# A convolution and expert-routing kernel on one core: smaller second matrices, normalising work spread to GpSimd, the choice of experts in two parts

## The chip, the core and the metric

The kernel runs on one core of a Trainium2 chip. The core has a matrix engine (PE; its weight loads are listed apart as PEld), VectorE (DVE in the profile), ScalarE (ACT), GpSimd (POOL) and SyncE (SP, which here only issues transfers). Each engine takes its own instructions strictly in order and waits for the others on semaphores. Transfers between the chip's memory and the on-chip memory run on 16 transfer engines; SP, ACT and POOL each have a queue that issues them.

The time is device microseconds of one execution. The metric is the median of several runs. A separate, profiled execution gives the trace.

## What is computed

The input is 32 images of 128 channels, 56 x 56. Layer 0, cut to what matters here:

```python
x = depthwise_conv7x7(input) + dw_bias            # each channel by itself
x = x.transpose(0, 2, 3, 1)                       # tokens: one per pixel, 128 channels
x = (x - mean) / sqrt(var + 1e-6) * ln_gamma + ln_beta
logits = x @ Wg + bg                              # 8 experts
topv, topi = top_k(logits, 2); wts = softmax(topv)
# tokens in order of falling wts[:, 0]; each expert keeps the first `cap` of them
h = gelu(buf @ W1 + b1); y = h @ W2 + b2          # per expert
out0 = input + x + layer_scale * (weighted sum of a token's two experts)
```

Layer 1 is a dilated 3 x 3 convolution, a two-dimensional Fourier transform, attention and a gate in the frequency domain, and the way back. The change touches nothing of it.

## The kernel before

The kernel has three parts in time: the **convolution stage** with the layer norm and the choice of experts (up to about 1073 us), the routing and the experts, and the last part with the combination and layer 1. Only the first is touched.

The convolution stage works on 8 **groups** of 4 images. A group has TG = 98 columns of 128 tokens; its result is the tile `y`, 128 tokens x 98 columns x 128 channels, of which two exist, so that one group can be finished while the next is filled. A group is filled in 16 **steps** (NS) of 8 channels (CB). Step `k` calls `conv` (L124): it loads `xt`, the pixels of 8 channels on 112 partitions (L127), and `wt`, the matrices of these channels (L129); both have three buffers. The 7 x 7 convolution of a channel is written as matrix products: 8 x 8 output pixels of a tile need 14 rows of input, which are cut into two **row blocks** of 8 rows; `b` = 0 and 1 are the two products that are added up (L136). A row block has 8 rows x 14 columns = 112 rows of a matrix (PK). In the second block, rows 6 and 7 of 8 carry only zeros. VectorE takes 4 channels at a time out of PE's result, adds the bias and writes `y` (L144): two evictions a step.

A filled group is worked off behind the steps of the next one, in seven **blocks** of columns (six of 16, one of 2). `block` (L152) has five phases:

- `stats`: VectorE's `bn_stats` per column (L161), a few small operations, ScalarE's square root (L172), reciprocal and bias (L173, L174);
- `norm`: ScalarE scales and shifts each column with its own two factors (L181), VectorE multiplies the whole block by gamma and adds beta (L185), ScalarE's queue issues the write to `xf` in memory (L188);
- `across`: PE transposes the columns (L196), ScalarE copies four at a time (L198);
- `logits`: PE multiplies by Wg (L206, L234), ScalarE copies (L215);
- `back`: PE transposes (L220), VectorE adds the bias into `lg` (L223, L243).

After the last block, `choose` (L252) finds the two largest logits of each token, in some 20 VectorE operations over all 98 columns (L263 to L302), ScalarE's exponential (L291) among them; it fills `meta`, a tile with a single buffer that GpSimd clears first (L288), and ScalarE's queue issues the write of `meta` to `xf` (L299), in pieces of 64 bytes, 12,544 of them. `key` (L302) stays on the chip.

`plan` (L314) sets the order: phase `i` of block `b` is put behind step `b * 3 // 2 + i` of the next group, and `choose` behind the step after the last phase, the fifteenth. The last group has no next one: its phases run one after another, the **tail** of the stage. After that, the order of instructions on each engine is made by the framework's scheduler, which moves instructions ahead where it finds room; waits follow from the tiles' use. PE's order keeps to the plan: the transposes of block 0 stand behind step 2 of the next group, those of blocks 1 to 6 behind steps 3, 5, 6, 8, 9 and 11. They wait for the normalised block, and the matmuls of the next step stand behind them.

The tiles of the next part lie where those of the stage lay, so its first instructions wait for the stage's last transfers; VectorE's memset of `onesj` (L470) waits for the last write of `meta`.

Of the kernel before, what the change touches and what calls it, by code (L numbers as in the profile page):

```python
# [29 lines left out]
F32 = mybir.dt.float32  # L30
I32 = mybir.dt.int32
AF = mybir.ActivationFunctionType
ALU = mybir.AluOpType
# [4 lines left out]
C = 128  # L38
# [6 lines left out]
E = 8  # L45
# [4 lines left out]
P8 = 8  # L50
NB = H // P8
NP = NB * NB
NCB = NB + 1
PK = P8 * (P8 + 6)
CB = 8
PITCH = 144
BIG = 1.0e30
# [14 lines left out]
def conv_seq_kernel(ctx: ExitStack, tc: tile.TileContext, t: dict, out: bass.AP, dbg: dict):  # L72
    nc = tc.nc
# [39 lines left out]
    TG = 2 * NP  # L113
    with tc.tile_pool(name="a1", bufs=1) as a1, tc.tile_pool(name="a2", bufs=2) as a2, tc.tile_pool(
# [9 lines left out]
        def conv(g, c0, y):  # L124

            xt = a3.tile([PK, CB, 4 * NCB * NB], F32, name="xt")
            nc.sync.dma_start(out=xt, in_=t["x8"][g, c0 // CB])  # L127
            wt = a3.tile([PK, CB, 2, P8 * P8], F32, name="wt")
            nc.sync.dma_start(out=wt, in_=t["wt"][c0 // CB])  # L129
            xv = xt.rearrange("k c (h n q) -> k c h n q", h=2, n=2)  # L130
            for c4 in range(0, CB, 4):
                ps = bank("psa")
                for c in range(4):
                    for b in range(2):
                        for h in range(2):
                            nc.tensor.matmul(  # L136
                                ps[h * 64 : (h + 1) * 64, c * TG : (c + 1) * TG],
                                lhsT=wt[:, c4 + c, b, :],
                                rhs=xv[:, c4 + c, h, :, b * NB : b * NB + NP],
                                start=(b == 0),  # L140
                                stop=(b == 1),
                            )
                cs = slice(c0 + c4, c0 + c4 + 4)
                nc.vector.tensor_tensor(  # L144
                    out=y[:, :, cs],
                    in0=ps[:, : 4 * TG].rearrange("p (c t) -> p t c", c=4),
                    in1=dwbB[:, cs].unsqueeze(1).broadcast_to([128, TG, 4]),
                    op=ALU.add,
                )

        def block(g, y, lg, t0, n):
# [26 lines left out]
            def norm():  # L178
                for i in range(n):
                    yi = y[:, t0 + i, :]  # L180
                    nc.scalar.activation(  # L181
                        yi, yi, AF.Identity, scale=sd[:, i : i + 1], bias=nb[:, i : i + 1]
                    )
                for w, op in ((gB, ALU.mult), (bB, ALU.add)):
                    nc.vector.tensor_tensor(  # L185
                        out=yb, in0=yb, in1=w.unsqueeze(1).broadcast_to([128, n, C]), op=op
                    )
                nc.scalar.dma_start(out=xfv[:, g * TG + t0 : g * TG + t0 + n, :C], in_=yb)  # L188
# [60 lines left out]

            return [stats, norm, across, logits, back]  # L250

        def choose(g, lg):  # L252

            cut = slice(g * TG, (g + 1) * TG)
            bE = [128, TG, E]
            tops, hots = [], []
            cand = a1.tile(bE, F32, name="cand", tag="cand")
            for r in range(2):

                top = a2.tile([128, TG], F32, name=f"top{r}", tag=f"top{r}")  # L260
                first = firsts[r][:, cut]
                hot = a1.tile(bE, F32, name=f"hot{r}", tag=f"hot{r}")
# [24 lines left out]
            meta = a1.tile([128, TG, PITCH - C], F32, name="meta", tag="meta")  # L287
# [26 lines left out]
        def plan(g, y):  # L314
# [907 lines left out]
def layouts(np, v):  # L1222
# [34 lines left out]
    def bn(v, g, b, m, bias):  # L1257
# [2 lines left out]
    return {  # L1260
        "xp": xp,
        "x8": x8.reshape(n // 4, C // CB, PK, CB, 4 * NCB * NB),
        "wt": wt.reshape(C // CB, PK, CB, 2, P8 * P8),
        "iota": np.arange(128 + n // 2 * NP, dtype=f),
        "reset": np.tile((np.arange(NB) > 0).astype(f), n // 2 * NB),
        "dw_bias": L0["dw_bias"],
# [41 lines left out]
```

## Time and profile before

| | us |
|---|---|
| median of 3 runs | 6502.28 (6499.15 to 6507.23) |
| the profiled execution | 6513.53 |
| its span in the trace | 6511.8 |
| PE busy (matmuls) | 4898.1 (75%) |
| VectorE busy | 3096.6 (48%) |
| GpSimd busy | 2601.1 (40%) |
| ScalarE busy | 2097.7 (32%) |
| first matmul of the convolution stage | at 12.41 |
| last eviction of the convolution stage | at 944.18 |
| end of the last write of `meta` | at 1073.25 |

Busy times are sums over an engine's instructions; a share of the whole span is a mean over parts with different limits, so each part has to be read by itself. The page cuts the span into 40 slices of about 163 us and prints the busy share of each in tenths. A timeline gives, for each piece: start, duration, engine, source line, operation, written tile and read tiles, count, and in brackets the idle time before it with what ended it. A wait is listed as "engine, tile, line <- what ended it: us in total, times, longest". The granted clock of PE in the stage is about 0.8 of full speed.

In the stage, per instruction: a matmul of L136 264 ns (mean), an eviction 565 ns, a ScalarE activation of one column 489 ns (one starts every 0.39 us), a VectorE multiplication or addition of a block of 16 columns 2290 and 2278 ns, a `bn_stats` 289 ns, a clearing of `meta` 1405 ns.

### The profile page before, as it was taken

How to read it: one execution, taken by the hardware profiler on the slowest of the kernel's cores; microseconds unless marked ns; L12 is line 12 of the kernel's file. 1: busy time of each engine (PE TensorE's matmuls, PEld its weight loads, DVE VectorE, ACT ScalarE, POOL GpSimd, SP SyncE). 2: the span in 40 equal slices, each digit the busy share in tenths (PEclk: the TensorE clock that was granted, in tenths of full speed). 3: DMA queues.
4: the chain of work that ended last, by engine and by line, in shares of the span. 5: the costliest groups of instructions: out<-in, count | busy, mean ns of one | idle time of the engine just before them, and what ended most of it. 6: DMA issues, size and time to landing. Idle time of an engine off the chain costs nothing.

```text
span 6511.8 us, 85508 instructions
## 1 busy us (share of the span) xinstructions
PE 4898.1 (75%) x32850; PEld 3362.9 (52%) x32850; DVE 3096.6 (48%) x6927; ACT 2097.7 (32%) x3595; POOL 2601.1 (40%) x2564
## 2 busy tenths in 40 slices
PE   6666652699898989999965677777777677767778
PEld 5555542476576756776742344443444444344445
DVE  4676675565665655535311343344344344434335
ACT  2445442133232323333310332233333233333225
POOL 0000000335343434544446555455555555655540
PEclk8878875799898999999986888888878888888889
DMA  8998973122121222222232233333333333323331
GB/s 230 224 227 221 231 186 75 45 62 69 50 69 52 69 55 68 71 67 71 73 110 59 63 91 89 83 92 81 83 93 89 85 94 96 84 72 96 88 86 43
DMA packets 616217, 634.09 MB, mean 97 GB/s; under 512 B 166145, under 2 KB 540546, under 8 KB 611714
## 3 DMA queue, kind: packets, MB, share of 16 engines
q1 hardware_dynamic: 332418, 395.64, 22.0%
q0 software_dynamic: 81664, 175.18, 11.7%
q10 hardware_dynamic: 201728, 57.81, 4.6%
q8 instruction: 260, 4.26, 0.3%
q14 instruction: 147, 1.20, 0.1%
HBM read 454.98 MB, written 173.41 MB: 97 GB/s over the span
## 4 chain that ended last, share of the span: by engine, by line
PE 36%; issue 15%; another core or an unknown queue 13%; POOL 8%; DVE 6%; DMA 2%; ACT 2%; DVEq 0%; POOLq 0%; SPq 0%; ACTq 0%
PE pf L895 8%; PE py L715 8%; PE ph L705 7%; POOL xg L671 6%; PE pm L939 6%; PE pt L931 3%; POOL y L850 2%; DMA xg<-xf,ids 2%; PE pg L964 2%; DVE mid L933 1%; PE pre L1030 1%; PE pim L1031 1%; PE pxt L677 1%; PE pxs L872 1%
## 5 line engine op out<-in xcount | busy, mean ns | idle before, releaser
L850 POOL DMA_INDIRECT y<-yf,slot x1568 | 1628.5, 1039 | 1403.0 <-DVE xs L864 764.8
L671 POOL DMA_INDIRECT xg<-xf,ids x984 | 961.1, 977 | 1380.9 <-PE pxt L677 519.7
L708 ACT ACTIVATE hT<-ph,b1t 128x512 f32<-128x512 f32 (+1 forms) x992 | 672.9, 682 | 1455.6 <-PE ph L705 1294.6
L715 PEld LDWEIGHTS py<-W,hT 128*128 128x128 f32 x7872 | 949.0, 194 | 241.0 <-issue 122.8
L895 PE MATMUL pf<-xp,cw 128*64 128x448 f32 x4032 | 988.2, 595 | 110.7 <-issue 69.5
L715 PE MATMUL py<-W,hT 128*128 128x128 f32 x7872 | 998.0, 281 | 88.9 <-DVE gat L682 42.0
L705 PE MATMUL ph<-xT,W 128*128 128x512 f32 (+1 forms) x1984 | 910.2, 597 | 8.8 <-issue 8.1
L933 DVE COPY mid<-pt 112x512 f32<-112x512 f32 (+3 forms) x480 | 312.6, 663 | 940.5 <-remote 413.3
L895 PEld LDWEIGHTS pf<-xp,cw 128*64 128x64 f32 x4032 | 315.8, 147 | 622.8 <-issue 547.7
L705 PEld LDWEIGHTS ph<-xT,W 128*128 128x128 f32 x1984 | 360.2, 194 | 349.9 <-issue 344.2
L136 PE MATMUL psa<-xt,wt 112*64 112x98 f32 x8192 | 416.5, 264 | 86.6 <-DMA wt<-in_wt_dram 80.9
L136 PEld LDWEIGHTS psa<-xt,wt 112*64 112x64 f32 x8192 | 392.9, 147 | 125.2 <-issue 59.4
L682 DVE SCALAR_TENSOR_TENSOR gat<-xg 128x4 f32<-128x4 f32 (+2 forms) x256 | 42.2, 165 | 763.9 <-DMA xg<-xf,ids 763.1
L288 POOL MEMSET meta<- 128x1568 f32 x8 | 11.2, 1405 | 951.1 <-DMA xf<-meta 360.8
L196 PE MATMUL pyt<-ident,y 128*128 128x128 f32 x784 | 154.3, 377 | 305.3 <-DVE nb L174 148.4
L877 DVE TENSOR_TENSOR xp<-xp,pxs 128x256 f32<-128x256 f32 x448 | 147.2, 385 | 489.0 <-remote 348.3
L942 ACT COPY T<-pm 128x464 f32<-128x464 f32 (+2 forms) x240 | 123.7, 520 | 617.1 <-PE pm L939 367.2
L939 PE MATMUL pm<-rh,mid 112*128 112x116 f32 x928 | 142.1, 298 | 236.5 <-issue 161.0
L181 ACT ACTIVATE y<-y,nb,sd 128x128 f32<-128x128 f32 x784 | 311.0, 489 | 18.5 <-DVE nb L174 18.5
L196 PEld LDWEIGHTS pyt<-ident,y 128*128 128x128 f32 x784 | 138.3, 201 | 331.8 <-issue 239.6
L864 DVE TENSOR_TENSOR xs<-xs,y 128x896 f32<-128x896 f32 x224 | 242.2, 1087 | 116.7 <-DMA y<-yf,slot 68.6
L144 DVE TENSOR_TENSOR y<-psa,dwbB 128x392 f32<-128x392 f32 x256 | 144.1, 565 | 317.0 <-PE psa L136 316.5
(376 smaller groups left out, 6498.0 us busy)
## 6 DMA issues: line engine op xcount, KB each, us to landing
xt<-in_x_dram SPq DMA_DIRECT2D x128, 784.0 KB
yf<-yo SPq DMA_DIRECT2D x240, 256.0 KB
xp<-in_xp_dram SPq DMA_DIRECT2D x32, 1832.0 KB
wt<-in_wt_dram SPq DMA_DIRECT2D x128, 448.0 KB
xs<-xf SPq DMA_DIRECT2D x112, 448.0 KB
xf<-y ACTq DMA_DIRECT2D x48, 1024.0 KB
y<-yf,slot POOLq DMA_INDIRECT x1568
out_dram<-oa SPq DMA_DIRECT2D x224, 112.0 KB
```

What stands on the lines that cost most here:

```text
L136: nc.tensor.matmul(ps[h * 64 : (h + 1) * 64, c * TG : (c + 1) * TG], lhsT=wt[:, c4 + c, b, :], rhs=xv[:, c4 + c, h, :, b * NB : b * NB + N ...
L181: nc.scalar.activation(yi, yi, AF.Identity, scale=sd[:, i : i + 1], bias=nb[:, i : i + 1])
L196: nc.tensor.transpose(pt[:, i * 128 : (i + 1) * 128], y[:, t0 + i0 + i, :], ident)
L671: nc.gpsimd.indirect_dma_start(out=xg[:n, q, :], out_offset=None, in_=xf, in_offset=bass.IndirectOffsetOnAxis(ap=ids[:n, c0 + q : c0 + q + ...
L705: nc.tensor.matmul(ph[:, :ns], lhsT=W1[:, e, f * C : (f + 1) * C], rhs=xT[:, :ns], start=True, stop=True)
L708: nc.scalar.activation(hT[:, f, :ns], ph[:, :ns], AF.Gelu, bias=b1t[:, e, f : f + 1])
L715: nc.tensor.matmul(py[:n, q * C : (q + 1) * C], lhsT=hT[:, f, q * 128 : q * 128 + n], rhs=W2[:, e, f, :], start=(f == 0), stop=(f == FF // ...
L850: nc.gpsimd.indirect_dma_start(out=y[:, m, :], out_offset=None, in_=yf, in_offset=bass.IndirectOffsetOnAxis(ap=s[:, r * NB + m : r * NB + ...
L864: nc.vector.tensor_tensor(out=xs, in0=xs, in1=y, op=ALU.add)
L895: nc.tensor.matmul(pf[i * DD : (i + 1) * DD, : 8 * W], lhsT=cw[:, k, :], rhs=xps[i][:, o : o + 8 * RP].rearrange("p (h w) -> p h w", w=RP) ...
L933: dve(mid[:m, :ni, :].rearrange("p i c -> p (i c)"), pt[:m, : ni * 128])
L939: nc.tensor.matmul(pm[:, i * M : (i + 1) * M], lhsT=mid[:m, i, :], rhs=by, start=True, stop=True)
```

## The change

It has three parts.

1. The matrices are two tensors, `wt0` with 112 rows and `wt1` with the 84 rows that are not all zero; each step loads both, and the second product uses 84 partitions of `xt`. A step's loads fall from 784 + 448 KB to 784 + 224 + 168 KB, in three transfers instead of two.
2. In `norm`, columns 1, 4, 7, 10 and 13 of a block (5 of 16; 1 in the last block of 2) are scaled and shifted by GpSimd instead of ScalarE, and the addition of beta is GpSimd's instead of VectorE's. The multiplication by gamma stays on VectorE, between the two.
3. `choose` is called twice a group: for the first three blocks (48 columns) behind step 8, for the other four (50 columns) behind step 14. Each call clears and writes its own part of `meta`; the tile has one buffer as before.

```diff
-            wt = a3.tile([PK, CB, 2, P8 * P8], F32, name="wt")
-            nc.sync.dma_start(out=wt, in_=t["wt"][c0 // CB])
+            wts = []
+            for b, k in enumerate(PKS):
+                wt = a3.tile([k, CB, P8 * P8], F32, name=f"wt{b}")
+                nc.sync.dma_start(out=wt, in_=t[f"wt{b}"][c0 // CB])
+                wts.append(wt)
...
-                                lhsT=wt[:, c4 + c, b, :],
-                                rhs=xv[:, c4 + c, h, :, b * NB : b * NB + NP],
+                                lhsT=wts[b][:, c4 + c, :],
+                                rhs=xv[: PKS[b], c4 + c, h, :, b * NB : b * NB + NP],
...
-                    nc.scalar.activation(
-                        yi, yi, AF.Identity, scale=sd[:, i : i + 1], bias=nb[:, i : i + 1]
-                    )
-                for w, op in ((gB, ALU.mult), (bB, ALU.add)):
-                    nc.vector.tensor_tensor(
+                    si, bi = sd[:, i : i + 1], nb[:, i : i + 1]
+                    if i % 3 == 1:
+                        nc.gpsimd.tensor_scalar(
+                            out=yi, in0=yi, scalar1=si, scalar2=bi, op0=ALU.mult, op1=ALU.add
+                        )
+                    else:
+                        nc.scalar.activation(yi, yi, AF.Identity, scale=si, bias=bi)
+                for w, op, eng in ((gB, ALU.mult, nc.vector), (bB, ALU.add, nc.gpsimd)):
+                    eng.tensor_tensor(
                         out=yb, in0=yb, in1=w.unsqueeze(1).broadcast_to([128, n, C]), op=op
                     )
...
-        def choose(g, lg):
+        def choose(g, lg, t0, t1):
...
-            last = max(at)
-            at[last + 1] = [lambda: choose(g, lg)]
+            half = sum(sizes[:3])
+            at.setdefault(8, []).append(lambda: choose(g, lg, 0, half))
+            at.setdefault((len(sizes) - 1) * 3 // 2 + 5, []).append(lambda: choose(g, lg, half, TG))
```

PE's order of products and transposes in the stage stays as it was, up to the tail. GpSimd, which had nothing in the stage but one clearing a group, now has in each group: the clearing of the second half's `meta`, the clearing of the next first half's, the five activations of block 0, its addition, those of block 1, its addition, ten activations (blocks 2 and 3), two additions, eleven activations (blocks 4 to 6), three additions. On VectorE most of the first half's choice stands between the multiplications of blocks 4 and 5. On ScalarE the write of the first half's `meta` is issued just before block 5's write of `y`.

More of the change, by code (lines that the diff above doesn't have):

```diff
@@ L54 @@
 PK = P8 * (P8 + 6)
+PKS = PK, 6 * (P8 + 6)
 CB = 8
@@ L250, in block @@
             return [stats, norm, across, logits, back]
-        def choose(g, lg):
-            cut = slice(g * TG, (g + 1) * TG)
-            bE = [128, TG, E]
+        def choose(g, lg, t0, t1):
+            n = t1 - t0
+            lg = lg[:, t0:t1, :]
+            cut = slice(g * TG + t0, g * TG + t1)
+            bE = [128, n, E]
             tops, hots = [], []
-            cand = a1.tile(bE, F32, name="cand", tag="cand")
+            cand = a1.tile([128, TG, E], F32, name="cand", tag="cand")[:, :n]
             for r in range(2):
-                top = a2.tile([128, TG], F32, name=f"top{r}", tag=f"top{r}")
+                top = a2.tile([128, TG], F32, name=f"top{r}", tag=f"top{r}")[:, :n]
                 first = firsts[r][:, cut]
-                hot = a1.tile(bE, F32, name=f"hot{r}", tag=f"hot{r}")
+                hot = a1.tile([128, TG, E], F32, name=f"hot{r}", tag=f"hot{r}")[:, :n]
                 nc.vector.tensor_reduce(out=top, in_=lg, axis=AX.X, op=ALU.max)
@@ L286, in choose @@
             m1, e1 = tops
-            meta = a1.tile([128, TG, PITCH - C], F32, name="meta", tag="meta")
+            meta = a1.tile([128, TG, PITCH - C], F32, name="meta", tag="meta")[:, :n]
             nc.gpsimd.memset(meta, 0.0)
@@ L1262, in layouts @@
         "x8": x8.reshape(n // 4, C // CB, PK, CB, 4 * NCB * NB),
-        "wt": wt.reshape(C // CB, PK, CB, 2, P8 * P8),
+        "wt0": wt[..., 0, :, :].reshape(C // CB, PK, CB, P8 * P8),
+        "wt1": wt[:, :6, ..., 1, :, :].reshape(C // CB, PKS[1], CB, P8 * P8),
         "iota": np.arange(128 + n // 2 * NP, dtype=f),
```

## The prediction

> **What bounds the kernel now.** I read the page's slices first, then the busy time by window, then the waits of the first 800 us, then the timeline of one period of the convolution stage. The built program is the old one after that stage, but for line numbers and a little order at its edge, so all gain or loss lies before 1073 us.
>
> ```profile
> DVE  4676675565665655535311343344344344434335
> ...
> DMA  8998973122121222222232233333333333323331
> ```
>
> The first five slices (163 us each) are the stage: the transfer engines are nearly full there and nowhere else, VectorE stands at about seven tenths. Close up, by windows of 100 us (columns: busy time of PE, weight loads, VectorE, ScalarE, GpSimd; granted clock; transfer share):
>
> ```profile
> 300.00:400.00 100.00, 64.44 (x978) 56.22 (x974) 71.41 (x211) 40.38 (x96) 1.41 (x1) 0.81 0.99 227
> 400.00:500.00 100.00, 62.46 (x950) 55.28 (x950) 71.80 (x198) 43.78 (x104) 1.40 (x1) 0.79 0.99 231
> ```
>
> No compute engine is full and the transfers look full, which suggests a stage bound by loads. The waits say otherwise:
>
> ```profile
> PE pyt L196 <- DVE nb L174: 100.6, 18, 13.3
> ...
> PE psa L136 <- DMA wt<-in_wt_dram: 71.2, 38, 12.4
> ...
> PE pyt L196 <- ACT y L181: 39.3, 5, 7.9
> ```
>
> PE waits longer for normalised rows (the transposes of L196) than for loads. The period from 336.8 to 459.4 us shows how both fit. After the last eviction of a group (336.83) come three loaded steps; then PE stands before the transposes of block 0 (they start at 362.67), and again before those of blocks 1 to 5, at 380.03, 391.98, 405.63, 418.81 and 428.88. Meanwhile the three buffers fill up and SP stops issuing (transfers fall to zero near 377 and 385 us). Steps 10 to 13 then run at PE's pace, and PE waits for loads only from 449.96 on, some 2 us a step. So a period is a **chain of blocks** (92 us) plus a stretch in which loads decide (30 us). The last link of the chain, word for word:
>
> ```profile
> 418.81 1.94 PE L196 MATMUL pyt<-ident,y 128*128 128x128 f32 x16 [1.02 <-DVE y L185]
> ...
> 423.64 0.57 DVE L144 TENSOR_TENSOR y<-psa,dwbB 128x392 f32<-128x392 f32 x1 [0.78 <-PE psa L136]
> 424.13 2.28 DVE L185 TENSOR_TENSOR y<-y,gB 128x2048 f32<-128x2048 f32 x1
> ...
> 426.44 2.29 DVE L185 TENSOR_TENSOR y<-y,bB 128x2048 f32<-128x2048 f32 x1
> ...
> 428.88 3.65 PE L196 MATMUL pyt<-ident,y 128*128 128x128 f32 x16 [4.29 <-DVE nb L174]
> ```
>
> Block 4's transposes, a step of matmuls, its two evictions, multiplication, addition, block 5's transposes: the addition stands in the chain with its full 2.29 us.
>
> **The addition on GpSimd.** No row shows GpSimd adding. Its memset of 128x1568 takes 1405 ns, 0.90 ns an element, so 2048 elements cost 1.84 us for one stream; two operands in and one out cost 5.5 us if streams follow each other. Bounds 1.84 and 5.5 us. I take 4.6, two and a half streams, since the row of its own engine is nearer than VectorE's 2.28. That is +2.3 us per block of 16. The Trainium skill's page GPSIMD Engine Reference, Performance versus the Vector engine, speaks against this move: it gives 4497 ns for this addition on GpSimd and 2293 on VectorE; the second agrees with 2.28 here, and by the first the difference would be 2.2 instead of 2.3, and the sum below 5 us smaller.
>
> **A third of the normalising.** ScalarE's row (L181, 128x128) starts one every 0.39 us; 11 instead of 16 save 1.95 us a block. GpSimd's five, at two streams of 128 and the 0.10 us of its smallest memsets, are about 0.35 each (bounds 0.2, and 0.49, ScalarE's mean), 1.75 us a block beside ScalarE.
>
> **The chain, link by link** (before, then after). *Last eviction to block 0*: 25.8. The second half's choice is half as long (below), so its meta write leaves at 337.4, not 343.88. But GpSimd's order puts the memset for the next group's first half, which waits for that write, ahead of block 0's five activations. Beside loads the write moved 7373 packets in 20 us, so 6400 need 17 us; GpSimd is free at 355.4, the five end at 357.2, multiplication 359.5, addition 364.2, transposes 364.3: 27.5. *0 to 1*: 17.4, set by copies, 16 activations (6.27), multiplication and addition. After, seven activations are left behind the copies, and the multiplication is set by the next step's evictions, at 8.0; with 2.3 and 4.7 it is 15.1. *1 to 2*: multiplication at 7.2 in both (behind L223), so 12.0 becomes 14.3. *2 to 3*: was set by 16 activations, now by an eviction at 5.4: 13.7 becomes 12.5. *3 to 4*: 13.2, plus 2.3 and a reduction of the first choice in VectorE's order: 15.6. *4 to 5*: 10.1 becomes 12.4. Sum 92.2 to 97.4: **+5.2** a period. ScalarE's relief shortens two links; in the others an eviction decides and the slower addition is paid in full.
>
> Beside the additions, VectorE now runs halves of the choice ahead of block 5's multiplication. No row has GpSimd reading tiles beside VectorE; its memsets take 1.40 us beside VectorE work as alone. Between nothing and a wait that costs 2 us (VectorE held for the addition's 4.6, less the slack in that link) I take **+0.5**; a gain is excluded, since neither engine gets less to do by it.
>
> **The loads.** One step moves 1232 KB; from 15 to 85 us, loads alone, 18.00 MB in 70 us make 4.9 us a step. 56 KB less is 0.22 us if all 16 transfer engines share it, nothing if some engine keeps seven rows. On rows of 2048 instead of 4096 bytes I put no price: the y writes, in rows of 512, run at up to 290 GB/s when alone (the slices of 960 to 1000 us), the loads at 259. About six steps a period wait for loads: -1.3 to 0. The page DMA: Bandwidth & Descriptors, Why a DMA increments its semaphore by 16 and not by 1, says that a transfer is split over the largest number up to 16 that divides its rows: 112 rows take 16 engines, 84 only 14, six rows each. By it the fullest engine falls from 78,848 to 76,800 bytes a step, 2.6% instead of 4.5%, or 0.13 us; no row here shows single engines. I take **-1.0**. SP's third issue a step (0.42 us) stands in a queue that mostly waits for PE.
>
> **The choice in two parts.** The same elements, twice the instructions: 16 more, some 0.1 us each, on a VectorE at 72% that loses 2.28 us a block. The first half's meta write moves from the chain, where transfers have gaps, into the loaded stretch. In 343 to 363 us the loads took 20 us for 17 us of work beside 7373 packets, 0.4 ns a packet: up to +2.5. Also, a y write issued behind a meta write holds ScalarE's queue:
>
> ```profile
> 343.88 0.37 ACTq L299 DMA_DIRECT2D xf<-meta  x1
> ...
> 362.60 4.34 ACTq L188 DMA_DIRECT2D xf<-y  x1
> ```
>
> 4.34 us instead of 0.37. After, block 5's y write is issued directly behind the first half's meta write, and its four copies, the logits and step 11 stand behind it: 0 to +4, partly taken up by PE's later waits. Both together, **+2.8**.
>
> Sum of a period: 5.2 + 0.5 - 1.0 + 2.8 = +7.5; seven periods +52.
>
> **The tail**, from the last eviction (944.18) to 1073.2. Block 0 is no longer behind the long choice: its transposes come 5 us earlier. The six links then lose half of that: -2.6 at block 5. The last choice took 1043.46 to 1057.29; at 0.57 instead of 0.97 us for each of its 13 large instructions it saves 6. The wait behind it,
>
> ```profile
> 1057.29 15.96 DMA xf<-meta
> ```
>
> falls with 6400 instead of 12544 packets to about 9: -7. Together **-15**.
>
> **Sum.** +52 - 15 = +37 us on the profiled 6513.53 (span 6511.8): 6550. That execution is 11 us above the median of 6502.28, so the median becomes **6540**.
>
> **Rivals.** *The addition is fast.* A microsecond of it is worth six links in seven periods and six in the tail, 48 us. Below 3.8 us the sum turns negative; at VectorE's 2.28 it would be -74, near the most that the gaps of the transfers (8 us a period) and the tail allow: 6430. For it speaks that memset's rate is no worse than VectorE's; against, that two operands must be read. 0.20. *All cancels*: the addition near 3.8, or the first half's write costs nothing: 6502. 0.10. *GpSimd is held*: its memset waits as long as now, when the whole meta write lands 24 to 26 us after its issue, so block 0 comes 8 us later still, and VectorE waits for additions: +10 a period, 6610. Against it, half the packets. 0.10. *The smaller matrices bring nothing* is inside the forecast: it costs 7 us.
>
> **Chances.** Forecast 0.60 (6516 to 6590). About 13 us, 0.2%, is what a measurement of this kernel can tell from no change. Faster 0.20, within 0.10, slower 0.70. With the addition's bounds the range is 6470 to 6600: it leaves out the fastest additions and the worst hold.
>
> **What would show it.** In the new profile: the addition's mean on GpSimd, about 4.6 us; transposes of blocks 2, 4 and 5 later after their forerunners by 2.3 us, those of 1 and 3 earlier; the period 129 us instead of 122; more transfer gaps though fewer bytes; the memset of 768 elements a microsecond or two before block 0's activations on GpSimd; block 5's y issue over 1 us; the stage's end some 37 us later, and nothing different behind it. An addition under 3.8 us, or a chain that still ends 92 us after the last eviction, makes it wrong.

## The result, and the profile after

| | us |
|---|---|
| before, median of 4 runs | 6504.75 (6499.15 to 6510.69) |
| after, median of 4 runs | 6566.01 (6549.64 to 6577.24) |
| ratio | 1.0092, 95% interval 1.0068 to 1.0116 |
| profiled execution of after, its span | 6564.6, 6562.8 |
| clearing of `onesj`, the stage's end | 1142.3 (before 1073.5) |

The change costs 61 us; 38 were forecast. The whole loss arises ahead of the stage's end, which comes 69 us later; the later parts, with the same instructions, give 18 us of it back in these two profiled executions, which are 51 us apart (by the medians it is 8 us). A second pair of runs on another chip gave 6581.52 against 6511.57, ratio 1.0105 (1.0052 to 1.0159), with the stage's end at 1147.3.

First the slices of the page of after, the counterpart of the two lines shown of before:

```profile
DVE  4767776656656555345221234443443344434336
...
DMA  8788774122222222222233233333333333333331
```

In the first five slices the transfers have fallen from eights and nines to sevens and eights: the stage moves 7 MB less and takes longer. VectorE is no less busy. By windows of 100 us (busy time of PE, weight loads, VectorE, ScalarE, GpSimd; granted clock; transfer share; GB/s), again for after:

```profile
300.00:400.00 100.00, 61.81 (x831) 54.05 (x827) 74.70 (x200) 26.96 (x60) 27.68 (x23) 0.76 0.81 195
400.00:500.00 100.00, 73.19 (x1055) 62.69 (x1056) 67.33 (x135) 33.21 (x73) 26.56 (x22) 0.83 0.81 208
```

VectorE finishes 335 instructions in 200 us, before 409, and is as busy: some of its instructions have become longer. The transfer share fell from 0.99 to 0.81. The stage now waits for its chain more than before, and the waits of the first 800 us of after say at what:

```profile
POOL meta L298 <- DMA xf<-meta: 236.7, 10, 42.1
...
PE pyt L204 <- POOL y L193: 216.6, 31, 14.9
ACT y L191 <- DVE nb L178: 152.7, 22, 13.2
...
PE psa L140 <- DMA wt<-in_wt_dram: 44.8, 37, 10.9
```

PE's transposes now wait for GpSimd's addition (L193); the wait for matrices has gone down from 71.2 to 44.8 us. New is the third line, ScalarE waiting for `nb` (L178), the bias of the next block's activations: 12 us between 200 and 900 us in before, 144 in after (15 in after with the addition back on VectorE, below).

From here, the **period** is the mean time from one group's last eviction to the next one's over the last six periods (before 121.9 us, after 134.1), and a **link** is the time from one block's transposes to the next one's. In the period of after that starts at 352.3:

| link to block | 0 | 1 | 2 | 3 | 4 | 5 | chain | behind it |
|---|---|---|---|---|---|---|---|---|
| before | 25.8 | 17.4 | 12.0 | 13.6 | 13.2 | 10.1 | 92.1 | 30.5 |
| forecast | 27.5 | 15.1 | 14.3 | 12.5 | 15.6 | 12.4 | 97.4 | 32.3 |
| after | 28.4 | 16.8 | 15.0 | 13.9 | 14.9 | 15.3 | 104.1 | 32.4 |
| before, mean of the six periods | 26.4 | 17.3 | 12.3 | 13.7 | 13.1 | 10.1 | 92.9 | 29.0 |
| after, mean of the six periods | 27.2 | 16.8 | 14.6 | 13.8 | 14.7 | 15.2 | 102.4 | 31.8 |

By the means the chain grew by 9.5 us and the stretch behind it by 2.7.

What VectorE and ScalarE do beside an addition stands in the timeline of after. Block 3's addition (421.72), its transposes (426.27) and the first of block 4's activations (426.28; start, duration, engine, line, operation, in brackets the idle time before and what ended it):

```profile
421.72 4.49 POOL L193 TENSOR_TENSOR y<-y,bB 128x2048 f32<-128x2048 f32 x1 [9.41 <-DVE y L193]
421.84 4.41 DVE L178 SCALAR_TENSOR_TENSOR nb<-nb,sd 128x16 f32<-128x16 f32 x1
...
426.27 3.62 PE L204 MATMUL pyt<-ident,y 128*128 128x128 f32 x16 [6.44 <-POOL y L193]
426.28 0.49 ACT L191 ACTIVATE y<-y,nb,sd 128x128 f32<-128x128 f32 x1 [5.72 <-DVE nb L178]
```

An operation on 16 elements takes 4.41 us instead of 0.15: VectorE starts it beside the addition and is done when the addition is done. All of VectorE's queue stands behind it, and so does ScalarE, which needs `nb`. The same happens beside each of the six additions of a period, to one operation each, by its place in VectorE's order:

```profile
408.22 4.10 DVE L170 TENSOR_TENSOR nb<-st 128x2 f32<-128x2 f32 x1
...
436.86 4.61 DVE L274 TENSOR_TENSOR cand<-lg,top 128x384 f32<-128x384 f32 x1
...
451.93 4.48 DVE L303 TENSOR_SCALAR top<-top 128x48 f32<-128x48 f32 x1
```

Not every operation is held. In the second profile of after, between 200 and 900 us, all 15 of the `nb` operations of 128x16 that met an addition took 4.4 us, the 15 others 0.15. But where the addition alone was moved (a run below, with `meta` cleared once), ten evictions lie wholly beside an addition, and took 0.50 to 0.57 as always; their first operand lies in PE's result memory. The Trainium skill's page SBUF — State Buffer, Who interferes with whom, says that a VectorE instruction with two inputs in SBUF contends with a GpSimd instruction that reads SBUF, not with one that only writes, and that the second to come waits for the whole of the first; it counts `tensor_scalar` among those that can contend too. The rows here agree with it. They show the other order too: block 5's addition, which began 0.07 us behind a VectorE operation on two tiles (128x384), took 4.83 us in all six periods, where the other blocks' took 4.49 to 4.54.

A hold lengthens the chain only where it stands on it. The chain that ended last in after, followed back from its end, shows this (start, us, engine and line; `x64` are the matmuls of a step), first in the link to block 1, then in those to blocks 3 and 5:

```profile
376.31 4.29 DVE nb L178
...
412.36 3.46 PE pyt L204 x16
415.82 3.03 PE psa L140 x64
...
419.36 2.29 DVE y L193
421.72 4.50 POOL y L193
426.27 3.62 PE pyt L204 x16
...
441.12 3.68 PE pyt L204 x16
444.79 3.87 PE psa L140 x64
...
449.17 2.29 DVE y L193
451.53 4.84 POOL y L193
```

Beside block 0's addition the held `nb` is on the chain. In the other links it is the addition itself, with its full 4.5 us, and the held operation beside it is not on the chain. This is so in all six periods of both profiles of after; in one period of each a second held operation stands there in the place of its addition, just as long.

The second thing that the chain shows is PE's pace. Block 2's 16 transposes take 3.46 us, where before they took 1.94; block 4's take 3.68 instead of 1.94 and the step behind them 3.87 instead of 2.92. In before PE had stood still for 0.6 and 1.0 us ahead of these transposes, in after for 2.7 and 3.3 us, since the addition is longer. In all fourteen profiles together, 16 transposes took 1.94 to 1.97 us where PE had stood at most 1.5 us ahead of them (126 blocks), and 2.4 to 3.7 us where it had stood 2.7 us or more (462 blocks). So a longer wait of PE can make the next link longer too.

### The profile page after: what moved, and what is told of

The parts are those of the page before. It is cut to its first block, busy times and chain, and to the rows that moved or that the text cites. A ratio compares the mean times of both kernels' runs of the same rounds, so it can differ in the third digit from the quotient of the medians.

```text
span 6562.8 us, 85985 instructions
## 1 busy us (share of the span) xinstructions
PE 4964.9 (76%) x32850; PEld 3407.5 (52%) x32850; DVE 3197.6 (49%) x7039; ACT 2002.6 (31%) x3357; POOL 2961.1 (45%) x2876
## 3 DMA queue, kind: packets, MB, share of 16 engines
q0 software_dynamic: 81664, 175.18, 12.4%
## 4 chain that ended last, share of the span: by engine, by line
PE 38%; issue 15%; another core or an unknown queue 14%; POOL 13%; DVE 10%; DMA 6%; ACT 3%; SPq 0%; DVEq 0%; POOLq 0%; ACTq 0%
PE pf L907 7%; POOL xg L683 7%; PE py L727 6%; PE pm L951 6%; PE ph L717 5%; PE pt L943 3%; PE psa L140 3%; POOL y L862 3%; POOL y L193 3%; PE pyt L204 2%; DMA wt<-in_wt_dram 2%; DMA xg<-xf,ids 2%; DVE y L193 2%; PE pg L976 2%
## 5 line engine op out<-in xcount | busy, mean ns | idle before, releaser
L862 POOL DMA_INDIRECT y<-yf,slot x1568 | 1652.1, 1054 | 1348.6 <-DVE xs L876 718.9
L907 PE MATMUL pf<-xp,cw 128*64 128x448 f32 x4032 | 986.3, 587 | 117.4 <-issue 113.4
L140 PE MATMUL psa<-xt,wt 84*64 84x98 f32 (+1 forms) x8192 | 442.6, 271 | 67.4 <-DMA wt<-in_wt_dram 49.2
L140 PEld LDWEIGHTS psa<-xt,wt 84*64 84x64 f32 (+1 forms) x8192 | 412.0, 153 | 113.7 <-issue 50.2
L204 PE MATMUL pyt<-ident,y 128*128 128x128 f32 x784 | 172.4, 408 | 348.1 <-POOL y L193 348.1
L193 POOL TENSOR_TENSOR y<-y,bB 128x2048 f32<-128x2048 f32 (+1 forms) x56 | 224.2, 4004 | 345.0 <-DVE y L193 345.0
L204 PEld LDWEIGHTS pyt<-ident,y 128*128 128x128 f32 x784 | 154.3, 219 | 377.7 <-POOL y L193 376.0
L191 ACT ACTIVATE y<-y,nb,sd 128x128 f32<-128x128 f32 x536 | 216.8, 484 | 218.0 <-DVE nb L178 218.0
L1030 ACT COPY Q<-pm 128x464 f32<-128x464 f32 (+1 forms) x128 | 63.9, 511 | 701.2 <-remote 461.9
```

What stands on the lines that cost most here:

```text
L140: nc.tensor.matmul(ps[h * 64 : (h + 1) * 64, c * TG : (c + 1) * TG], lhsT=wts[b][:, c4 + c, :], rhs=xv[: PKS[b], c4 + c, h, :, b * NB : b ...
L193: eng.tensor_tensor(out=yb, in0=yb, in1=w.unsqueeze(1).broadcast_to([128, n, C]), op=op)
L204: nc.tensor.transpose(pt[:, i * 128 : (i + 1) * 128], y[:, t0 + i0 + i, :], ident)
L862: nc.gpsimd.indirect_dma_start(out=y[:, m, :], out_offset=None, in_=yf, in_offset=bass.IndirectOffsetOnAxis(ap=s[:, r * NB + m : r * NB + ...
L907: nc.tensor.matmul(pf[i * DD : (i + 1) * DD, : 8 * W], lhsT=cw[:, k, :], rhs=xps[i][:, o : o + 8 * RP].rearrange("p (h w) -> p h w", w=RP) ...
```

## The experiments

The kernel before took about 5625 us on some of the chips used here and about 6510 on the others; the difference lies behind 3400 us, where the granted clock was 0.93 to 0.95 against 0.81, and the periods of the stage are the same. So each run is compared with before on its own chip, and the traces by the stage alone.

### The four parts, each alone on the kernel before

The addition alone:

```
-                for w, op in ((gB, ALU.mult), (bB, ALU.add)):
-                    nc.vector.tensor_tensor(
+                for w, op, eng in ((gB, ALU.mult, nc.vector), (bB, ALU.add, nc.gpsimd)):
+                    eng.tensor_tensor(
```

> Before, with the beta addition alone moved to GpSimd. My theory, from the trace of after: the addition costs twice, by its own length (4.55 us instead of 2.28, in each of six links of the chain) and because VectorE starts nothing to its end (single small operations of 4.1 to 4.6 us beside it). ScalarE's relief is missing here, so each link keeps its old length and gets 2.3 us, and up to 2.4 more where an eviction or a multiplication is due beside the addition: 14 to 20 us a period, together +105 to +145 us. A rival by which VectorE is not held would give the 2.3 us alone, +95 to +105. A rival by which the queue of meta writes is the cost would give at most +40 here. In the profile: the period 136 to 142 us instead of 122.

Measured: 5774.23 against 5627.77 us, ratio 1.0259 (1.0242 to 1.0276); period 142.1, stage end 1219.9, +146 us. The size fits, but not the reason: the link to block 0 grew by 13 us (39 instead of 26), the other five together by 9 us, less than five times the 2.27 us of added length. The 13 us come from here (the profile of this run, GpSimd's clearing of `meta`):

```profile
260.16 1.41 POOL L288 MEMSET meta<- 128x1568 f32 x1 [62.03 <-DMA xf<-meta]
...
403.77 1.40 POOL L288 MEMSET meta<- 128x1568 f32 x1 [59.88 <-DMA xf<-meta]
```

The clearing for the next choice waits until the last choice's write has left the only `meta` buffer, 34 us after the last eviction (226.6 and 369.7), and block 0's addition stands behind it on GpSimd.

The choice in two parts alone (the hunks of `choose` and `plan` of the change, nothing else):

> Before, with the choice in two parts alone. My theory: it costs little, since the hold of block 5's y write behind the first half's meta write (4.25 us in after) is taken up by later waits, and the tail's choice gets shorter: within -15 and +15 us. The rival that the moved meta write and the held ScalarE queue are the cost of after: +50 us or more, with the stretch from block 5 to the next group's last eviction 5 us or more longer than the 30.5 us of before.

Measured: 5616.9 us, ratio 0.9969 (0.9947 to 0.9991), period 122.5, stage end 1065.0: the last eviction comes 4.5 us later, and the tail is 13 us shorter. The rival falls.

Five of 16 activations alone (the hunk with `i % 3 == 1`):

> Before, with five of 16 activations of each block alone moved to GpSimd. My theory: ScalarE's relief shortens the links to blocks 1 and 3 by 2 us each, but GpSimd's memset of the whole meta now stands ahead of block 0's activations and waits for the whole meta write (landing 24 to 26 us after its issue at 7 us), so block 0's transposes come some 10 to 15 us later: +5 to +11 us a period, +35 to +80 us together. The rival that ScalarE's relief decides: -20 to -40 us. A third possibility, that GpSimd's activations hold VectorE as its addition does, would add up to 2 us a link more: +100 us and over.

Measured: 5637.41 us, ratio 1.0013 (1.0003 to 1.0024), stage end +5. My expectation of +35 to +80 falls: the hold was as expected, the relief was underrated. The link to block 0 was 39 to 44 us (before 26), the period 128.0. But the links to blocks 3 and 5 went down to 7 to 8 and 7.3 us (before 13.7 and 10.1), the second period, the only one with blocks in which no write of `meta` is yet in flight, took 106.0 us (before 123.0), and the tail lost 14.5 us. So the relief of ScalarE is worth much, and the memset's place in GpSimd's order eats it.

The smaller matrices alone (the hunks with `PKS`, `wts`, `wt0` and `wt1`):

> Before, with the second row block's matrices on 84 partitions in a tensor of their own, alone. My theory, from the first loads of after (4.96 us a step of 1176 KB instead of 4.91 us for 1232 KB): the loads got no faster, so -7 to +10 us. The forecast's term would give -7; loads that went with their bytes -10 or more. The rival that the new tensors slow the loads beside other traffic: +20 us and over. Behind the stage, after's two later parts took 14 us more and 33 us less than before's with the same instructions: if the placement of the tensors does that, it shows here too; if it varies between executions, it does not repeat.

Measured: 5626.82 us, ratio 1.0 (0.9987 to 1.0013), period 121.7, stage end +3: nothing. The +14 and -33 us that after's later parts had shown against before's do not come back with the new tensors.

The four differences add up to +144 us, the whole change costs 61 to 70: the parts share the wait behind the memset, which the choice in two parts shortens.

### The change itself again, and without single parts

> The changed kernel itself, on the chip of these runs, where the kernel before takes 5628 us and only the last part of the program is shorter than in the first profiles. All theories: +60 to +75 us, since the convolution stage of the parts made alone has the same periods on both chips (122 us for the matrices alone, as in the first profile of before).

Measured: +70 us, as told above; period 134.7.

After, with the addition back on VectorE:

```
-                for w, op, eng in ((gB, ALU.mult, nc.vector), (bB, ALU.add, nc.gpsimd)):
-                    eng.tensor_tensor(
+                for w, op in ((gB, ALU.mult), (bB, ALU.add)):
+                    nc.vector.tensor_tensor(
```

> After, with the beta addition back on VectorE. My theory now, from the links of the parts made alone: the addition costs the chain of after some 20 us a period, since the activations on GpSimd alone bring the links to blocks 3 and 5 to 7 us (13.9 and 15.3 in after). Then the period falls from 134 to 112 to 117 us, and the time to 70 to 40 us below before. The forecast's own terms (2.3 us of addition in six links, 0.5 for VectorE) would give 10 us a period less, about before's time or 10 us under it. The rival that the choice in two parts or the matrices are the cost: still 40 us and more above before.

Measured: 6497.07 against 6511.57 us, ratio 0.9976 (0.9952 to 0.9999), 84 us below after on the same chip: the addition on GpSimd is what turns the change into a loss. The chain is what I expected, 85.6 us (26.9, 14.7, 15.2, 8.3, 13.1, 7.4 for most groups), 18.5 shorter than in after (17.1 by the means of the six periods).

Most of that, 13.7 of 17.1 us, lies in the links to blocks 3 and 5, and there VectorE's instructions have another order. Here block 3's multiplication (the first line) starts at block 2's transposes (390.09), ahead of the evictions of the next step (the second line), and block 5's stands so too; PE goes from block 2's transposes through one step straight to block 3's:

```profile
390.06 2.28 DVE L193 TENSOR_TENSOR y<-y,gB 128x2048 f32<-128x2048 f32 x1
...
396.10 0.57 DVE L148 TENSOR_TENSOR y<-psa,dwbB 128x392 f32<-128x392 f32 x1 [0.97 <-PE psa L140]
```

In after block 3's multiplication (419.36) stands behind both evictions of that step (417.51 and 418.88), so transposes, step, multiplication and addition follow each other. The 17 us are therefore the price of the addition with the order that the scheduler made for it. Its own length accounts for at most 6 x 2.27 = 13.6 us; no run has after's order with the addition on VectorE, and why the scheduler orders so is not shown.

But the period fell only to 122.4: the stretch behind the chain grew from 32 to 37 us. The reason is on ScalarE's queue, behind the first half's write of `meta` (timeline of this run; "ACTq" is the issue of a transfer):

```profile
425.61 0.37 ACTq L309 DMA_DIRECT2D xf<-meta  x1
...
427.14 15.11 ACTq L196 DMA_DIRECT2D xf<-y  x1
...
442.29 0.37 ACT L206 COPY yT<-pyt 128x256 f32<-128x256 f32 x1 [14.76 <-issue]
...
442.71 1.02 PE L242 MATMUL pl<-wg,yT 128*128 128x8 f32 x4 [9.58 <-ACT yT L206]
```

The issue of block 6's small y write takes 15.11 us; its copy, PE's product for the logits and the next steps of matmuls wait. In after it is block 5's y write that stands there, 4.2 to 4.3 us in every group. This is the forecast's cost of the choice in two parts, with another transfer behind it and at three times the price.

After, with `meta` cleared once ahead of the stage:

```
+        metas = a1.tile([128, TG, PITCH - C], F32, name="metas", tag="meta")
+        nc.gpsimd.memset(metas, 0.0)
...
-            meta = a1.tile([128, TG, PITCH - C], F32, name="meta", tag="meta")[:, :n]
-            nc.gpsimd.memset(meta, 0.0)
+            meta = metas[:, t0:t1]
```

> After, with the meta tile cleared once ahead of the stage instead of before each half of a choice (only its first three columns are ever written, the others stay zero), so GpSimd has no memset that waits for a meta write. My theory: the first link of the chain falls from 28 to about 22 us, the others stay: 5 to 6 us a period, 35 to 45 us below after, so still 15 to 35 us above before. The rival that the wait behind the memset is the main cost of the change: back to before's time or under it.

Measured: 6553.9 against 6511.57 us, ratio 1.0051 (1.0021 to 1.0081), 28 us below after. First link 20.6 to 23.7 us, the others unchanged, period 129.1. The wait behind the memset is 5 to 6 us a period of after and not its main cost.

The addition alone, with `meta` cleared once (both edits above, `meta` undivided):

> The beta addition alone on GpSimd, and the meta tile cleared once. The addition alone took a first link of 39 us instead of 26, and that I put down to GpSimd's memset, which stands ahead of block 0's addition and waits for the meta write. Without it: first link 27 to 29 us, the other links as in the addition alone (16.8, 14.4, 16.1, 14.6, 13.8), period 129 to 131 us, 55 to 75 us above before instead of 146. If the first link stays near 39, something else holds it.

Measured: 6625.9 against 6511.57 us, ratio 1.0157 (1.0093 to 1.022); stage end +104. First link 28 to 31.5 us, so the memset was what held it, but the link to block 1 went from 16.8 to 18 and the period came to 135.1, where I had expected 129 to 131: without the hold the addition alone costs 13 us a period. Its links are longer than before's by 14 us in sum, about six times 2.27. There, evictions often come first in VectorE's order and pass; a held operation is on the chain once in five of the six periods, behind block 0 as in after.

### A memset of the same length in the place of the addition

After, with a memset of bytes instead of the addition:

```
-                    eng.tensor_tensor(
-                        out=yb, in0=yb, in1=w.unsqueeze(1).broadcast_to([128, n, C]), op=op
-                    )
+                nc.vector.tensor_tensor(
+                    out=yb, in0=yb, in1=gB.unsqueeze(1).broadcast_to([128, n, C]), op=ALU.mult
+                )
+                nc.gpsimd.memset(yb[:, :, :80].bitcast(mybir.dt.uint8), 63)
```

> After, with GpSimd's addition replaced by one memset of bytes over channels 0 to 79 of the block: it writes and reads nothing. It leaves the beta addition out and overwrites those channels. The chain still goes through GpSimd. If the memset takes 0.9 ns for each of its 5120 bytes it is as long as the addition (4.55 us). My theory: VectorE is not held beside it (the small operations there take 0.15 to 0.6 us instead of 4.1 to 4.6), and of the 18 us that the addition costs the chain (104 us, 85.6 without it) what is left is the difference in length alone: with 4.5 us six times 2.3, chain 97 to 100 us, period 127 to 131, 20 to 50 us below after; with a shorter memset as much less as it is shorter. The rival that the hold costs nothing: chain 102 us or more with a memset of 4.5 us. If VectorE is held beside a memset too, the hold does not come from the addition's reads.

Measured: GpSimd is occupied nearly as long, 4365 ns for one memset beside 4551 for one addition (groups of GpSimd in the two runs, busy time and mean ns of one):

```profile
L195 POOL MEMSET y<- 128x5120 uint8 x48 | 209.1, 4365 | 180.8 <-DVE y L192 179.9
```

```profile
L193 POOL TENSOR_TENSOR y<-y,bB 128x2048 f32<-128x2048 f32 x48 | 218.4, 4551 | 341.8 <-DVE y L193 341.8
```

and VectorE works beside it (timeline with the memset; two memsets, 8.67 us):

```profile
366.90 8.67 POOL L195 MEMSET y<- 128x5120 uint8 x2 [7.04 <-DVE y L192]
...
367.43 0.15 DVE L170 TENSOR_TENSOR nb<-st 128x2 f32<-128x2 f32 x1
...
368.78 2.29 DVE L192 TENSOR_TENSOR y<-y,gB 128x2048 f32<-128x2048 f32 x1 [0.93 <-ACT y L191]
```

The operation of L170 that took 4.10 us in after takes 0.15, and so it is with the others on two tiles: what holds them in after goes with the addition's reading. VectorE is not free beside a memset either: the copy of 48 elements into `meta`, 0.20 us in after, met a memset in seven groups and took 1.6 to 3.0 us in each, to the memset's end.

The period is 114.7 us instead of 134, the stage ends at 1000.2, 142 us before that of after; the chain is 82 to 86 us, far below the 97 to 100 that I had expected. (The whole, 6505.38 us, ratio 0.9989 with 0.9966 to 1.0013, says nothing here: other values of y make other choices, and the later parts do other work.) This is not the price of the hold, since the order of VectorE's instructions is another one here too: the multiplications of blocks 1, 3 and 5 stand ahead of the evictions of the step behind the transposes of the block before (block 3's, the last line above, stands even ahead of block 2's transposes, 371.32). Their links are 8.9, 7.7 and 8.1 us, about as short as those to blocks 3 and 5 with the addition on VectorE (8.0 and 7.3), and in after 16.8, 13.8 and 15.2. The run shows that GpSimd's 4.4 us need not lengthen these links when the block is multiplied early. What the hold alone costs in after's order no run shows; by the chain above it is one held operation a period.

### Versions without the addition on GpSimd

Before, with five of 16 activations on GpSimd and `meta` cleared once:

> Before, with five of 16 activations of each block on GpSimd and the meta tile cleared once. In the activations alone the links behind the first were 14.5, 15.5, 7.5, 13.1, 7.3 us (before 17.4, 12.0, 13.7, 13.2, 10.1), and the first was 41 for the memset that waits for the meta write; in the one period without such a wait (the second) the period was 106 us instead of 122. My theory: first link 22 to 27 us, period 106 to 114, so 55 to 110 us below before. The rival, for which the transfers speak (share 0.95 to 0.99 in before; the period of after without the addition stayed at 122.6 although its chain was 6 us shorter): the transfers hold the period at 120 to 122 us, and the time stays within 20 us of before.

Measured: 6451.11 against 6512.82 us, ratio 0.9906 (0.9876 to 0.9936); period 113.7, stage end 994.7, 79 us earlier. My theory holds, and the rival of a floor at 120 to 122 us falls. Two windows of this run:

```profile
300.00:400.00 100.00, 67.16 (x1005) 58.72 (x1000) 78.70 (x210) 44.68 (x105) 13.87 (x31) 0.83 1.03 243
400.00:500.00 100.00, 68.96 (x1014) 59.87 (x1014) 72.50 (x210) 38.05 (x89) 13.39 (x30) 0.81 0.99 228
```

The transfers read as busy all the time, so they may be what the chain meets next; no run shows that.

The same with the choice in two parts:

> The same with the choice in two parts: after without the addition on GpSimd, without the smaller matrices and without the memset's wait. In after without the addition, the issue of block 6's small y write stood 15.1 us on ScalarE's queue behind the first half's meta write, and one step of each period took 16 us for it. My theory: that hold is what the choice in two parts costs once the addition is gone, so it shows here too, and the period is 115 to 122 us, 5 us or more longer than with the whole choice. The rival that the smaller matrices (rows of 2 KB) held that period: no longer than with the whole choice, since the first link is shorter.

Measured: 6469.68 us, ratio 0.993 (0.9903 to 0.9958); period 117.8, stage end 1030.0, 35 us later than with the whole choice (the medians are 19 us apart, and the intervals of the ratios overlap). The chain is even shorter (80 us, since block 0 comes earlier), but one step of every period takes 16 to 17 us, and ScalarE's queue is held 15.8 to 17.3 us in front of block 6's y write, with the large matrices as with the small ones. The rival falls.

The fastest one with the smaller matrices (the edit of the matrices alone, on top):

> The fastest version so far (five of 16 activations on GpSimd, meta tile cleared once, whole choice, beta on VectorE) with the smaller matrices of the change. There the transfers are busy all the time (share 0.99 to 1.03 from 200 to 600 us, period 113 us), so that a lighter load could show what the chain hid before. My theory: the loads alone (15 to 85 us) took 4.9 to 5.1 us a step with 1232 KB and 5.0 to 5.1 with 1176 KB, so nothing: within 0.2% of the version without them, some 60 us below before. The rival that the step follows its bytes: 0.22 us a step, 3.5 us a period, 25 us lower. The rival that three transfers a step with rows of 2 KB cost: some 20 us higher.

Measured: 5553.66 against 5624.33 us, ratio 0.9869 (0.9846 to 0.9892), 71 us below before. Its interval overlaps that of the version with the large matrices, and the stages agree: period 113.4 against 113.7, stage end 997.2 against 994.7. Even where the transfers are busy all the time (share 0.99 to 1.01), 56 KB less a step bring nothing. Both versions beat before and after.

## Where the prediction held and where not

The direction and the place were right: slower, in the chain of blocks, nothing lost behind the stage. By steps:

- *The addition takes 4.6 us.* Measured 4.55, as much as the 4497 ns of the Trainium skill's page GPSIMD Engine Reference, Performance versus the Vector engine, that stood beside the estimate. The rival "the addition is fast" is out.
- *The links that an eviction decides.* Here the sum was too small. The forecast let block 3's multiplication start 5.4 us after block 2's transposes and gave block 5's link its old 10.1 us and the 2.3 of the addition, as if PE kept its pace. But with the longer addition PE waits longer, and then runs the transposes of blocks 2 and 4 in about 3.4 and 3.7 us instead of 1.94. The links to blocks 3 and 5 took 13.8 and 15.2 us where 12.5 and 12.4 were forecast: 4.1 of the 5.0 us by which the chain (102.4 by the means) is longer than the forecast sum of 97.4.
- *VectorE held beside it: +0.5, bounds 0 to 2 a period.* The mechanism is there, but not as priced: I had foreseen one wait, at block 5; there are six a period, each to the end of the addition, and what is held is often `nb`, without which ScalarE can't begin the next block. On the chain stands one of them, behind block 0's addition: the link to block 1 took 16.8 us, 1.7 more than forecast, inside the bounds. That this hold is the whole 1.7 is read from the chain and not shown by a run.
- *ScalarE's relief shortens two links.* It does not show in after: the links to blocks 1 and 3 were forecast to fall to 15.1 and 12.5 us and are 16.8 and 13.8 (before 17.3 and 13.7). That the forecast less 2.3 us a link (58.4 us for links 1 to 5) agrees with after with the addition back on VectorE (58.7) is luck: there the links to blocks 3 and 5 are 7 to 8 us, by the other order of VectorE's instructions. GpSimd's activations took 0.47 us each, forecast 0.35.
- *GpSimd held at block 0 by the memset.* Right: link 28.4 (27.2 by the means), forecast 27.5, and 21 to 24 without the memset. The timeline of after reads as foreseen, memset and five activations, then multiplication (373.70) and addition (376.07):

```profile
370.77 0.74 POOL L298 MEMSET meta<- 128x768 f32 x1 [42.11 <-DMA xf<-meta]
...
371.50 2.16 POOL L187 TENSOR_SCALAR y<-y,sd,nb 128x128 f32<-128x128 f32 x5
```

- *The loads, -1.0 a period.* Measured 0. In the loads alone, from 15 to 85 us, the versions with large matrices moved 17.2 to 18.0 MB and those with small ones 16.0 to 17.0, which is 4.9 to 5.1 and 5.0 to 5.3 us a step. The bytes went down and the time did not; no run tells apart whether the shorter rows or the third transfer a step took the gain back, and none shows the split over 14 engines.
- *The choice, +2.8.* In after the stretch behind the chain is 32.4 us in the period of the table, forecast 32.3 with the loads; by the means it grew by 2.7 us, forecast 1.8 with the loads, which gave nothing. The issue of block 5's y write is held as foreseen, as long as block 0's was in before:

```profile
457.99 0.37 ACTq L309 DMA_DIRECT2D xf<-meta  x1
458.45 4.24 ACTq L196 DMA_DIRECT2D xf<-y  x1
```

  That a hold of 15 us takes its place once the addition is gone was not foreseen.
- *The tail, -15.* Measured -8.9 (120.4 us from the last eviction to `onesj`, before 129.3). Block 0's transposes came 5.9 us earlier, forecast 5, but block 5's 1.2 later instead of 2.6 earlier: the additions are in these links too. The chain of after has a held `nb` there for 4.22 us (from 1036.91); that of the second profile has not, and its block 5 comes no earlier (91.1 us behind the last eviction, against 90.8). The old chain's wait of 15.96 us for the last write of `meta` has no line in the new one, but the write's issue at 1129.56 and `onesj` at 1142.35 leave 12.8 us for it, where 9 were forecast.
- *The rival "GpSimd is held".* Its first half, block 0 8 us later still, did not come. Its second, VectorE waiting for the additions, did come, beside all six, but it stands on the chain once a period. The time lies between the forecast and this rival.

In sum: seven periods were forecast 7.5 us longer, the last six are 12.2 longer; 78 us at the last eviction instead of 52, less 8.9 in the tail. So direction, place and the main mechanism, the slower addition paid in each link, were right, and the size was low.

Two rows of the old profile, both shown ahead of the result, held the missing term: block 4's transposes, 1.94 us after a wait of 1.02, and block 5's, 3.65 after a wait of 4.29. I did not ask which pace PE would have when the waits grew. For the hold I leaned on GpSimd's memset, which took 1.40 us beside VectorE's work as alone; it reads nothing and could not show what an operation does that reads.

## What to carry to other kernels

Before an elementwise operation goes to a slower engine, follow the chain: here the addition went from 2.28 to 4.55 us on it, in every link, and the longer wait made PE slower behind it. Then look at what VectorE has in its order beside a GpSimd operation with two inputs: a small operation on two tiles stands to the end of it, and the engine that needs its result stands too; whether that costs time depends on whether it is on the chain (here once of six). Work with one input and per-column factors (the activations here) went over at 0.47 us each, and with it, and `meta` cleared once, the period of before could be cut by 8 us. Look next at what stands ahead on the engine that gets the work: a clearing that waited for a transfer, harmless while GpSimd had nothing else to do, cost 13 to 15 us in each period once block 0's work stood behind it, and clearing the tile once removed it. A part that alone costs nothing (the choice in two parts) ended the stage 35 us later in a version whose chain is shorter, so the parts are to be tried on the version that is kept. And when a change of one instruction also changes the scheduler's order, the difference of two runs is the price of both.

## What the runs showed of the hardware

- VectorE beside GpSimd's addition: operations on two SBUF tiles, of 2 to 384 elements, to the addition's end, mostly 4.1 to 4.6 us instead of 0.15 to 0.56, and a `tensor_scalar` of 48 elements 4.48; evictions out of PE's result memory 0.50 to 0.57, unchanged. Beside a memset of 4.37 us the small ones on two tiles were unchanged, but a copy of 48 elements took 1.6 to 3.0 us instead of 0.20 and, in one group of the stage, a `tensor_scalar` of 48 elements 3.98 instead of 0.18. Beside GpSimd's activations of one column, small operations took up to 0.40 instead of 0.17.
- PE's 16 transposes of 128x128 (f32) took 1.94 to 1.97 us where PE had stood at most 1.5 us ahead of them, 2.4 to 3.7 where it had stood 2.7 us or more.
- A memset of bytes on GpSimd costs by the element: 4365 ns for 5120 bytes, 0.85 ns each, close to the 0.90 of the 4-byte elements of `meta`.
- The issue of a y write on ScalarE's queue behind a write in pieces of 64 bytes took 4.2 to 4.3 us in after and 4.5 to 5.3 in the choice alone when it was block 5's (1024 KB), and in the versions with the choice in two parts and the addition on VectorE 14.6 to 17.3 us in nearly every group when it was block 6's (128 KB) behind block 5's and `meta`. Why the small one waits longer stays open; another queue for `meta` was not tried.
